# Strassen skips that end in the states' PSUM group, a planner that replays its plans, and moved units in a hybrid attention kernel

## Chip, cores and metric

The kernel runs on one core of one Trainium2 chip. The metric is the device time of one execution in microseconds (us); less is better. Everything is float32. TensorE (PE) multiplies matrices into PSUM, VectorE (DVE), ScalarE (ACT) and GpSimd (POOL) do the elementwise work, and SyncE (SP) issues the DMA transfers.

## What is computed

The input is `X` of shape (4, 1024, 256): 4 batches, 1024 tokens, 256 features. Four residual blocks follow one another:

```
x = x + attention(layernorm(x))          # causal, one head of 256
x = x + mix(layernorm(x))
x = x + state_space(layernorm(x))        # 16 states
x = x + mix(layernorm(x))                # the same weights again

mix(x):  xr, xk = blends of x with the token before, by mu_r and mu_k
         out = sigmoid(xr @ W_r.T) * (square(relu(xk @ W_k.T)) @ W_v.T)

state_space(x):
    xn = layernorm(x) * ln_g + ln_b
    x_proj, z = split(xn @ W_in.T + b_in);  z = silu(z)
    B_proj = x_proj @ W_B.T * mean(dt)                # 16 states
    x_mean = causal convolution of B_proj with the decays
    y = (x_mean @ W_C.T + D_skip * x_proj) * z        # the skip is D_skip * x_proj
    return y @ W_out.T + b_out + x
```

## The kernel before, in words

The tokens are cut into 8 halves `j` of 512 tokens (batch `b = j // 2`). Activations are kept by features, as [128 partitions, 2, 512], so that one product of a weight block [128, 128] with 512 tokens fills one PSUM bank.

**A written order on TensorE, a planned one elsewhere.** The program does not emit its instructions directly. It fills a log (`Order`): `o.unit` is a piece of TensorE work, and the units run in the order in which they are logged; `o.op` is a piece of work for another engine or a DMA, with its needs and the engines that may do it. `Order.finish` (L179) gives each op a due time, computed backwards from the units, and then simulates the whole program (`_run`) for 20 plans of three parameters, each in up to 5 rounds. After a round, `_hurry` pulls forward the due times of what TensorE waited for in it (`self.waits`). The plan with the earliest simulated end is emitted. So the order on DVE, ACT, POOL and SP over the whole program depends on which plan wins. The planner knows PSUM as 4 single banks ("bank") and 2 pairs of banks ("pair"), and the time that DVE and POOL share a port as `port`.

**The stages.** Attention works by tiles `i` of 128 queries, 32 in all: scores `sc` (L1492), exponents, a turn by DRAM (`exps`, `pblocks`), the weighted sum `po` (L1597). `attend_prepare(n)` logs the layernorm of half `n`, its trip through DRAM (`rows_a`, `blocks_a`) and the transposes into `xa`; the loop over `i` calls it 8 or 12 tiles ahead. The first mix block (`mix1`, tiles ending in `_f`) is threaded between the tiles. Then come, by hand in one list: the gates z, the inputs of the states, the convolution (`pc`, L1798), which goes to DRAM as `m_dram` and comes back as `xmT`, and the skips and outputs, with the second mix block (`mix2`, tiles ending in `_g`) threaded behind. `outputs(j)` is the product with `W_out` for half `j` and logs the layernorm and blends that half `j` of `mix2` needs.

**Seven products.** A product of a 256x256 weight with a batch's two halves is eight block products. `seven_products` (L818) does it with seven by Strassen's scheme in Winograd's form: sums of weight blocks (`x_sums`) and of activations (`T1` to `T4`, from `stream_sums`) are multiplied, and DVE adds the products out of PSUM in a chain: `u1`, `u2`, `u3`, then the four result blocks. For the gates z of batches 1 to 3 it has the keys `zs1` to `zs3` (p_zs in the profile), for the skips `ss1` to `ss3` (p_ss), for the keys of `mix2` `gks0` to `gks2`. `all_gates` is an iterator over the gates and skips, and each step of `more_gates(n)` logs n of its units. Batch 0 does its skips plainly: `skip(0)` and `skip(1)` (L1848) open an accumulation in a pair of banks, and `mix_states(0)` (L1925) adds the states' share `W_C` there and closes it.

**The states' share.** For batches 1 to 3 `mix_states_apart(b)` (unit `pm{b}`, L1889) multiplies `xmT` with `w_c` on four row groups at once into two pairs. Then DVE adds the skip to it (`grown`, L1899), and POOL or DVE multiplies with z (`gated`, L1903).

Of the kernel before, what the change touches and what calls it, by code (L numbers as in the profile page):

```python
# [4 lines left out]

# [10 lines left out]
ALU = mybir.AluOpType  # L16
# [36 lines left out]
class Order:  # L53
# [23 lines left out]
        for share, margin in ((0.2, 2.5), (0.1, 1.5), (0.3, 4.0), (0.2, 1.5), (0.1, 2.5))  # L77
        for wait in (0.0, 0.08, 0.15, 0.22)
    ]
    ROUNDS = 5  # L80
    TRIALS = 4
    BANKS = {"bank": 4, "pair": 2}
# [95 lines left out]
    def finish(self):  # L178
        dues = self._due()  # L179
        self.made = {e["key"]: n for n, e in enumerate(self.log) if e["key"] is not None}  # L180
        self.ends = []
        best = math.inf
        for plan in self.PLANS:
            self.due = list(dues)
            for k in range(self.ROUNDS):
                used = list(self.due)
                end = self._run(plan, False)
                self.ends.append((end, k, plan))
                if end < best:
# [4 lines left out]
        self._run(plan, True)  # L194

    def _hurry(self, key, wait):

# [8 lines left out]
    def _run(self, plan, emits):  # L206
        self.SHARE, self.MARGIN, self.WAIT = plan
        self.emits = emits
        self.waits = []
        self.now = self.at = 0.0  # L210
        self.free, self.ready, self.offered = {}, {}, []
        self.queue = self.port = 0.0
        self.waiting = {}
        self.psum = {kind: [0.0] * k for kind, k in self.BANKS.items()}
        for n, e in enumerate(self.log):
            if e["kind"] == "op":
                self._enter(n)
            elif e["kind"] == "known":
                self._done(e["key"], e["time"])
            elif e["kind"] == "take":  # L220
                heapq.heappop(self.psum[e["takes"]])
            else:
                self._unit(e)
        while self.offered:
            self._step()
        return max(self.now, *self.free.values())
# [57 lines left out]
    def _step(self):  # L284
        self.at, k = self._first()
        time, n = self.offered.pop(k)
        e = self.log[n]
        end, _, engine, emit = self._way(time, n)
        engine, _, port = engine.partition("+")
        self.free[engine] = end  # L290
        if port or engine == "POOL":
            self.port = end
        if self.emits:
            emit()
        if e["frees"]:
            heapq.heappush(self.psum[e["frees"]], end + self.LAG)
        if e["moves"]:
            for k, work in enumerate(e["moves"]):
                issued = end - (len(e["moves"]) - 1 - k) * self.log[n]["cost"] / len(e["moves"])
                self.queue = max(self.queue, issued + self.FLIGHT) + work  # L300
            self._done(e["key"], self.queue + self.LANDING)
        else:
            self._done(e["key"], end + e["lag"])
# [46 lines left out]
def hybrid_kernel(  # L350
# [1515 lines left out]
    def skips_of_batch(b):  # L1866

        there = columns_of(2 * b) + columns_of(2 * b + 1)
        src = lambda h, xb=(xnT[2 * b], xnT[2 * b + 1]): xb[h]()
        for j in (2 * b, 2 * b + 1):  # L1870
            skips[j] = lazy(lambda j=j: cols(f"skip_{j}"))
        sb = [skips[2 * b], skips[2 * b + 1]]
        sums_of_batch(b + 1)
        yield from seven_products(
            f"ss{b}", f"zs{b}", wx_block, lambda k: x_sums[:, k - 1, :], src, sums_of_batch(b),
            lambda e, h: sb[h]()[:, e, :], lambda e: b_skip[:, e : e + 1],
            ["x_sums", "b_all"], there,
        )

    def mix_states_apart(b):  # L1880

        for h in range(2):
            py[2 * b + h] = lazy(lambda h=h: pair(f"py_{2 * b + h}"))

        def emit():
            for e in range(KC):
                for h in range(2):
                    k = 2 * e + h
                    nc.tensor.matmul(  # L1889
                        py[2 * b + h]()[:, ts(e, HALF)],  # L1890
                        lhsT=w_c[k * GRP : k * GRP + S, ts(e, P)],
                        rhs=xmT[b]()[k * GRP : k * GRP + S, ts(h, HALF)],
                        start=True,
                        stop=True,
                    )

        def grown(j, e):
            t = skips[j]()[:, e, :]
            nc.vector.tensor_add(t, py[j]()[:, ts(e, HALF)], t)  # L1899

        def gated(engine, j, e):
            t = z[j]()[:, e, :]
            engine.tensor_mul(t, t, skips[j]()[:, e, :])  # L1903

        o.unit(f"pm{b}", 1.0, ["w_c", f"xmT{b}"], emit, "pair", many=2)
        for h in range(2):
            j = 2 * b + h
            for e in range(KC):
                o.op(
                    f"g{e}.{j}", [f"pm{b}", f"ss{b}.c{e + 1}{h + 1}"],  # L1910
                    ("DVE", dve(HALF) + 0.03, partial(grown, j, e)),
                    frees="pair" if e else None,
                )
# [107 lines left out]
    for i in range(-2, NI):  # L2021
        first, second = mix_units(i)
        while scored < min(i + (2 if i < AHEAD_FROM else 3), NI - 1):
            scored += 1
            if scored % NT == 0:
                for _ in chain:
                    pass
            scores(scored)
            if scored >= TURNED_BY_DRAM:
                turn_by_dram(scored)  # L2030
        go_on(APART)
        for unit in first:
            unit()
        go_on(APART)
        if 0 <= i + 1 < TURNED_BY_DRAM:
            turn(i + 1)
        j, k = divmod(i + 4, 4)
        if i == 0:
            next(attend_transpose(1))
        if 0 < j < 2 * NB:  # L2040
            if k == 0 and j == 1:
                attend_prepare(2)
            for n in range(3, 2 * NB):

                if i == 4 * n - (12 if n % 2 and n > 2 * SEVEN_FROM else 8):
                    attend_prepare(n)
            if k == (1 if i < AHEAD_FROM else 0) and j < 2 * SEVEN_FROM:
                both(queries, j)
            if k == 3 and j % 2 == 1 and SEVEN_FROM <= j // 2 + 1 < NB:
                chain = queries_of_batch(j // 2 + 1)  # L2050
                behind = len(o.log)
        while valued < min(i + (3 if i < AHEAD_FROM else 4), NI - 1):
            valued += 1
            values(valued)
        go_on(APART)
        for unit in second:
            unit()
        go_on(APART)
        if i == 10:
            decay_powers([f"e{i}", "la", "dtc", "dtr"])  # L2060
        if i == 13:
            decay_table()
        if 20 <= i < 23:
            next(steps_of_weights)
        if i >= 0:
            weigh(i)
            go_on(APART)
            if i % NH == NH - 1:
                mix1.prepare(i // NH, by_hand=i == NI - 1)
# [67 lines left out]
    more_gates(4)  # L2137
    outputs(2)
    more_gates(4)
    mix_states_apart(2)  # L2140
    outputs(3)
    more_gates(3)
# [86 lines left out]
```

## Time and profile before

| | |
|---|---|
| median of 3 runs | 465.42 us (465.42 to 465.47) |
| the profiled execution | 465.0 us, its span 463.1 us |
| granted TensorE clock | 1.0 |
| PE / DVE / ACT / POOL busy | 456.0 / 390.2 / 220.8 / 143.1 us |
| moved by DMA | 69.44 MB, mean 150 GB/s |

Attention and the first mix block take about the first 280 us, the gates, states and convolution go to about 310 us, the skips, outputs and the second mix block fill the rest. In the profile a float32 product of [128, 128] with 512 columns appears as two matmul instructions. A row that says "x8" has merged eight instructions, its second number runs from the first start to the last modelled end, and its last matmul still drains while the next row's first one runs, so that the rows overlap. "A <- B" after a row in brackets is idle time and what ended it. L numbers are lines of the kernel.

### The profile page before, as it was taken

The numbers are of one execution on the slowest core, as the hardware profiler recorded it, in microseconds if no ns is written. First come the engines' busy times: TensorE is split into PE (matmuls) and PEld (weight loads), VectorE is DVE, ScalarE is ACT, GpSimd is POOL, SyncE is SP. The second block draws the span as 40 slices with busy tenths as digits, with TensorE's granted clock in tenths as the row PEclk, the third lists the DMA queues.
The fourth block names the chain that finished last, engine by engine and source line by source line (L and its number), as shares of the span: only waits on it lengthen the run. The fifth ranks groups of instructions, "written<-read, shape, count | busy, mean of one in ns | idle before, by whom it ended". The sixth has DMA issues, their size and how long they took to land.

```text
span 463.1 us, 6634 instructions
## 1 busy us (share of the span) xinstructions
PE 456.0 (98%) x2052; PEld 312.5 (67%) x2052; DVE 390.2 (84%) x931; ACT 220.8 (48%) x463; POOL 143.1 (31%) x149
## 2 busy tenths in 40 slices
PE   8999999999999999999999999999999999999996
PEld 5766785667786667786777775474565758675875
DVE  3687769899969999889999977459889999999962
ACT  3422414454342433333556567441458777664652
POOL 3000102112013213121271354962052616826340
PEclk9999999999999999999999999999999999999999
DMA  8047876848455763427866989603022024252442
GB/s 242 21 127 203 250 190 168 222 132 258 117 135 139 221 194 93 118 62 237 224 177 182 275 268 271 260 17 88 11 92 91 1 86 144 81 147 99 129 144 84
DMA packets 84915, 69.44 MB, mean 150 GB/s; under 512 B 20160, under 2 KB 82576, under 8 KB 84880
## 3 DMA queue, kind: packets, MB, share of 16 engines
q1 hardware_dynamic: 84064, 68.76, 50.8%
q10 hardware_dynamic: 816, 0.26, 0.2%
q8 instruction: 16, 0.26, 0.2%
q14 instruction: 19, 0.16, 0.1%
HBM read 40.54 MB, written 28.45 MB: 149 GB/s over the span
## 4 chain that ended last, share of the span: by engine, by line
PE 86%; DVE 8%; issue 2%; DMA 1%; POOL 1%; ACT 1%; SPq 0%; DVEq 0%; POOLq 0%
PE po L1597 13%; PE sc L1492 13%; PE pv L1464 5%; PE p_zs L830 4%; PE p_ss L830 4%; PE p_qs L830 2%; PE p_gks L830 2%; PE py L1848 2%; PE pc L1798 2%; PE dust L1282 1%; DMA blocks_a<-rows_a 1%; PE pr_g0.pr L881 1%; PE pb L1735 1%; PE pp_a0.pq L774 1%; PE pr_g0.pv L881 1%
## 5 line engine op out<-in xcount | busy, mean ns | idle before, releaser
L1597 PE MATMUL po<-v,prT 128*128 128x256 f32 x288 | 67.7, 380 | 0.1
L1492 PE MATMUL sc<-xa,q 128*128 128x512 f32 (+3 forms) x192 | 67.0, 486 | 0.0
L1597 PEld LDWEIGHTS po<-v,prT 128*128 128x128 f32 x288 | 54.2, 189 | 11.6 <-issue 2.6
L1513 ACT ACTIVATE pr<-pr,nmx 128x128 f32<-128x128 f32 (+7 forms) x32 | 24.7, 773 | 64.6 <-DVE pr L1508 57.7
L1492 PEld LDWEIGHTS sc<-xa,q 128*128 128x128 f32 x192 | 35.1, 190 | 24.5 <-issue 19.6
L1464 PE MATMUL pv<-wv,xa 128*128 128x257 f32 x128 | 32.9, 380 | 0.0
L642 POOL TENSOR_TENSOR rs_a<-ve_a,minus_half 128x4 f32<-128x4 f32 x7 | 7.1, 1010 | 76.8 <-DVE ve_a L629 76.8
L1044 POOL TENSOR_TENSOR x<-x,r_f 128x512 f32<-128x512 f32 x16 | 20.3, 1271 | 33.0 <-DVE r_f L1038 32.5
L642 POOL TENSOR_TENSOR rs_h<-ve_h,minus_half 128x8 f32<-128x8 f32 x8 | 13.2, 1647 | 52.5 <-DVE ve_h L631 52.5
L1464 PEld LDWEIGHTS pv<-wv,xa 128*128 128x128 f32 x128 | 23.6, 191 | 7.8 <-issue 3.6
L1508 DVE TENSOR_SCALAR_CACHE_REDUCE pr<-sc,v 128x128 f32<-128x128 f32 (+7 forms) x32 | 26.2, 818 | 1.1
L1550 DVE STREAM_TRANSPOSE prT<-pblocks 128x384 f32<-128x384 f32 (+7 forms) x30 | 23.8, 793 | 2.4 <-DMA pblocks<-exps 2.3
L642 POOL TENSOR_TENSOR rs_f<-ve_f,minus_half 128x4 f32<-128x4 f32 x8 | 8.4, 1053 | 47.1 <-DVE ve_f L629 28.8
L1044 POOL TENSOR_TENSOR x<-x,r_g 128x512 f32<-128x512 f32 x14 | 18.9, 1371 | 11.0 <-DVE r_g L1038 11.0
L1641 POOL TENSOR_TENSOR x<-x,bout_r 128x512 f32<-128x512 f32 x16 | 20.0, 1279 | 4.5 <-ACT x L1634 4.5
L1606 DVE SCALAR_TENSOR_TENSOR x<-po,rsm,x 128x256 f32<-128x256 f32 x32 | 15.0, 470 | 4.3 <-PE po L1597 3.8
L1474 DVE TENSOR_TENSOR v<-pv,bv_r 128x257 f32<-128x257 f32 x32 | 13.4, 418 | 5.6 <-PE pv L1464 5.6
L930 DVE SCALAR_TENSOR_TENSOR xr_g<-hT_g,mur,xr_g 128x512 f32<-128x512 f32 x16 | 17.3, 1112 | 0.0
L663 ACT ACTIVATE xn_f<-x,mrs_f,rs_f 128x256 f32<-128x256 f32 x18 | 9.8, 592 | 15.5 <-DVE mrs_f L651 15.5
L1634 ACT ACTIVATE x<-x,mrs_h,rs 128x256 f32<-128x256 f32 x32 | 16.9, 592 | 0.0
L1903 POOL TENSOR_TENSOR z<-z,skip 128x512 f32<-128x512 f32 x9 | 13.1, 1462 | 10.9 <-DVE skip L1899 10.7
L663 ACT ACTIVATE xn_g<-x,mrs_g,rs_g 128x256 f32<-128x256 f32 x23 | 12.4, 589 | 8.3 <-DVE mrs_g L626 6.7
(458 smaller groups left out, 1089.8 us busy)
## 6 DMA issues: line engine op xcount, KB each, us to landing
hk<-r_dram SPq DMA_DIRECT2D x16, 512.0 KB, 9.2
rows_g<-xn_g SPq DMA_DIRECT2D x8, 512.0 KB, 2.9
blocks_g<-rows_g SPq DMA_DIRECT2D x32, 128.0 KB, 2.8
x<-in_L_attn_a_X_dram SPq DMA_DIRECT2D x7, 512.0 KB, 4.9
rows_f<-xn_f SPq DMA_DIRECT2D x7, 512.0 KB, 3.0
blocks_f<-rows_f SPq DMA_DIRECT2D x28, 128.0 KB, 2.7
rows_h<-xn_h SPq DMA_DIRECT2D x7, 512.0 KB, 3.7
blocks_h<-rows_h SPq DMA_DIRECT2D x28, 128.0 KB, 3.2
```

The costliest lines, as they stand in the source:

```text
L642: nc.gpsimd.tensor_tensor(rs()[:, :k].rearrange("p k n -> p (k n)"), ve()[:, :k].rearrange("p k n -> p (k n)"), minus_half[:, : k * NH], A ...
L663: nc.scalar.activation(place(n), split(row(n)), AF.Identity, bias=mrs()[:, k - 1, n : n + 1], scale=rs()[:, k - 1, n : n + 1],)
L830: lambda: nc.tensor.matmul(p(), lhsT=w(), rhs=data(), start=True, stop=True), "bank",
L930: nc.vector.scalar_tensor_tensor(t()[:, c, :], hT()[:, c, :HALF], mu1[:, c : c + 1], t()[:, c, :], ALU.mult, ALU.add,)
L1044: nc.gpsimd.tensor_add(xg, xg, r()[:, ts(g, 2), :])
L1464: nc.tensor.matmul(pv()[:, : D + 1], lhsT=xaj()[:, c, ts(n, P)], rhs=wv[:, c, :], start=(c == 0), stop=(c == KC - 1),)
L1492: nc.tensor.matmul(sc()[:, k * HALF : k * HALF + w], lhsT=qh()[:, c, ts(n, P)], rhs=keys[k]()[:, c, :w], start=(c == 0), stop=(c == KC - 1),)
L1508: nc.vector.tensor_scalar(dst, src, v[2 * b + h]()[:, n, D : D + 1], None, ALU.add, ALU.min, accum_out=nmx(),)
L1513: nc.scalar.activation(p()[:, :nk], p()[:, :nk], AF.Exp, bias=nmx(), scale=-1.0, accum_out=sm())
L1550: nc.vector.transpose(dst()[:, : NH * width].rearrange("p (k m a) -> p k m a", m=NH, a=GRP), blocks().rearrange("p m (k a) -> p k m a", a= ...
L1597: nc.tensor.matmul(po()[:, :D], lhsT=src()[:, ts(n, P)], rhs=v[2 * b + n // NH]()[:, n % NH, :D], start=(n == 0), stop=(n == t),)
L1641: nc.gpsimd.tensor_add(xg, xg, bout_r.unsqueeze(1).to_broadcast([P, 2, D]))
```

## The change

**The skips of batches 1 to 3.** `skips_of_batch` no longer runs all seven products. It runs four (1, 6, 7 and 5), and DVE makes from them `u1`, `u2 = u1 + p6`, `u3 = u2 + p7`, `u5 = u3 + p5` and `u4 = u2 + p5`, written straight into the four blocks of `skip`. The other three products (2, 4 and 3) move into the unit `pm{b}` of `mix_states_apart`, where each opens the accumulation group of one result block in the pairs; the states' share is then added onto it in PSUM. The fourth block has no product of its own and is opened by the states' share. `grown` then adds PSUM, the bias and the block `u` in one instruction. As the skips now have 4 steps instead of 7, all counts of `more_gates` change.

**The planner.** After each simulated run, the plan is replayed six times in its fixed order with varied durations (DVE up to 3% longer, ACT up to 4%, POOL up to 25%, each DMA landing up to 0.6 us later). The mean end of the replays decides between plans, and the waits averaged over the replays are what `_hurry` works on.

**Places.** `attend_prepare(n)` for n = 4 to 7 is logged one tile earlier. `skip(0)` moves from behind `state_inputs(1)` to ahead of `state_transpose(7)`. `mix2.gates(3, 0)` moves from behind the seven keys' products of batch 1 to between the fourth and the fifth; `mix2.gates(3, 1)` stays behind the seventh.

```diff
@@ class Order
+    SAMPLES = 6
+    SPREAD = {"DVE": 0.03, "ACT": 0.04, "POOL": 0.25}
+    LATE = 0.6
...
-                end = self._run(plan, False)
+                self._run(plan, False)
+                end = self._replays()
...
+    def _replays(self):
+        lost, ends = {}, 0.0
+        for k in range(self.SAMPLES):
+            rng = random.Random(k)
+            ends += self._replay(rng, lost)
+        self.waits = [(key, t / self.SAMPLES) for key, t in lost.items() if t > 0.1 * self.SAMPLES]
+        return ends / self.SAMPLES
+
+    def _replay(self, rng, lost):
...
+            spread = self.SPREAD.get(engine, 0.0)
+            at += cost * (1.0 + spread * rng.random())
...
+                at = queue + self.LANDING + self.LATE * rng.random()
...
@@ skips_of_batch(b)
-        yield from seven_products(
-            f"ss{b}", f"zs{b}", wx_block, lambda k: x_sums[:, k - 1, :], src, sums_of_batch(b),
...
+        u1, u2, u3, u5 = block(0, 0), block(0, 1), block(1, 0), block(1, 1)
+        p = unit(1, lambda: wx_block(0, 0), lambda: xnT[2 * b]()[:, 0, :], there)
+        o.op(f"{key}.u1", [f"{key}.p1"], *copies(u1, p), frees="bank")
+        yield
+        p = unit(6, lambda: x_sums[:, 1, :], lambda: T(2), [f"zs{b}.T2"])
+        add("u2", 6, p, u1, u2, "u1")
+        yield
+        p = unit(7, lambda: x_sums[:, 2, :], lambda: T(3), [f"zs{b}.T3"])
+        add("u3", 7, p, u2, u3, "u2")
+        yield
+        p = unit(5, lambda: x_sums[:, 0, :], lambda: T(1), [f"zs{b}.T1"])
+        add("u5", 5, p, u3, u5, "u3", last=False)
+        add("u4", 5, p, u2, u2, "u3")
+        yield
@@ mix_states_apart(b)
+            for h, e, w, data in (
+                (0, 0, wx_block(0, 1), xnT[2 * b]()[:, 1, :]),
+                (0, 1, wx_block(1, 1), T(4)),
+                (1, 0, x_sums[:, 3, :], xnT[2 * b + 1]()[:, 1, :]),
+            ):
+                nc.tensor.matmul(
+                    py[2 * b + h]()[:, ts(e, HALF)], lhsT=w, rhs=data, start=True, stop=False
+                )
...
-                        start=True,
+                        start=(k == 3),
...
-            nc.vector.tensor_add(t, py[j]()[:, ts(e, HALF)], t)
+            nc.vector.scalar_tensor_tensor(
+                t, py[j]()[:, ts(e, HALF)], b_skip[:, e : e + 1], t, ALU.add, ALU.add
+            )
...
-        o.unit(f"pm{b}", 1.0, ["w_c", f"xmT{b}"], emit, "pair", many=2)
+        o.unit(
+            f"pm{b}", columns(HALF, 3) + 1.05,
+            ["w_c", "x_sums", "b_all", f"xmT{b}", f"zs{b}.T4"] + there, emit, "pair", many=2,
+        )
@@ the loop over tiles
-                if i == 4 * n - (12 if n % 2 and n > 2 * SEVEN_FROM else 8):
+                if i == 4 * n - (12 if n % 2 and n > 2 * SEVEN_FROM else 8) - (n > 3):
                     attend_prepare(n)
@@ the list behind attention
     more_gates(5)
+    skip(0)
     state_transpose(7)
     state_inputs(0)
     more_gates(3)
     state_inputs_rows(0)
     state_inputs(1)
-    skip(0)
+    more_gates(2)
     state_inputs_rows(1)
-    more_gates(3)
+    more_gates(1)
...
     skip(1)
-    more_gates(8)
+    more_gates(6)
     mix_states(0)
-    more_gates(8)
+    more_gates(5)
     outputs(0)
-    more_gates(5)
+    more_gates(3)
     mix_states_apart(1)
     outputs(1)
-    more_gates(4)
+    more_gates(3)
     outputs(2)
-    more_gates(4)
+    more_gates(3)
     mix_states_apart(2)
     outputs(3)
     more_gates(3)
...
     outputs(7)
-    advance(keys, 7)
-    both(mix2.gates, 3)
+    advance(keys, 4)
+    mix2.gates(3, 0)
+    advance(keys, 3)
+    mix2.gates(3, 1)
```

More of the change, by code (lines that the diff above doesn't have):

```diff
@@ L2 @@
 import math
+import random
 from contextlib import ExitStack
@@ L194, in finish @@
         self._run(plan, True)
+    def _replays(self):
[6 more added lines that the diff above has]
+    def _replay(self, rng, lost):
+        now = queue = port = 0.0
+        free, ready = {}, {}
+        psum = {kind: [0.0] * k for kind, k in self.BANKS.items()}
+        for n, way in self.trail:
+            e = self.log[n]
+            if e["kind"] == "known":
+                ready[e["key"]] = e["time"]
+                continue
+            if e["kind"] == "take":
+                heapq.heappop(psum[e["takes"]])
+                continue
+            last, at = None, 0.0
+            for k in e["needs"]:
+                if ready[k] > at:
+                    last, at = k, ready[k]
+            if e["kind"] == "unit":
+                for _ in range(e["many"] if e["takes"] else 0):
+                    at = max(at, heapq.heappop(psum[e["takes"]]))
+                if last is not None and at > now + 0.1:
+                    lost[last] = lost.get(last, 0.0) + at - now
+                now = max(now, at) + e["cost"]
+                ready[e["key"]] = now + self.LAG
+                continue
+            engine, shared, cost = way
+            if e["moves"]:
+                at = max(at, queue - self.FLIGHT - 0.5)
+            at = max(at, free.get(engine, 0.0), port if shared or engine == "POOL" else 0.0)
+            spread = self.SPREAD.get(engine, 0.0)
+            at += cost * (1.0 + spread * rng.random())
+            free[engine] = at
+            if shared or engine == "POOL":
+                port = at
+            if e["frees"]:
+                heapq.heappush(psum[e["frees"]], at + self.LAG)
+            if e["moves"]:
+                for k, work in enumerate(e["moves"]):
+                    issued = at - (len(e["moves"]) - 1 - k) * e["cost"] / len(e["moves"])
+                    queue = max(queue, issued + self.FLIGHT) + work
+                at = queue + self.LANDING + self.LATE * rng.random()
+            else:
+                at += e["lag"]
+            if e["key"] is not None:
+                ready[e["key"]] = at
+        return max(now, *free.values())
     def _hurry(self, key, wait):
@@ L208, in _run @@
         self.emits = emits
-        self.waits = []
+        self.waits, self.trail = [], []
         self.now = self.at = 0.0
@@ L218, in _run @@
             elif e["kind"] == "known":
+                self.trail.append((n, None))
                 self._done(e["key"], e["time"])
             elif e["kind"] == "take":
+                self.trail.append((n, None))
                 heapq.heappop(self.psum[e["takes"]])
@@ L223, in _run @@
                 self._unit(e)
+                self.trail.append((n, None))
         while self.offered:
@@ L287, in _step @@
         e = self.log[n]
-        end, _, engine, emit = self._way(time, n)
+        end, start, engine, emit = self._way(time, n)
         engine, _, port = engine.partition("+")
+        self.trail.append((n, (engine, port, end - start)))
         self.free[engine] = end
@@ L1868, in skips_of_batch, with block, unit, add @@
         there = columns_of(2 * b) + columns_of(2 * b + 1)
-        src = lambda h, xb=(xnT[2 * b], xnT[2 * b + 1]): xb[h]()
+        key = f"ss{b}"
+        T = sums_of_batch(b)
         for j in (2 * b, 2 * b + 1):
             skips[j] = lazy(lambda j=j: cols(f"skip_{j}"))
-        sb = [skips[2 * b], skips[2 * b + 1]]
         sums_of_batch(b + 1)
-        yield from seven_products(
-            f"ss{b}", f"zs{b}", wx_block, lambda k: x_sums[:, k - 1, :], src, sums_of_batch(b),
-            lambda e, h: sb[h]()[:, e, :], lambda e: b_skip[:, e : e + 1],
-            ["x_sums", "b_all"], there,
-        )
+        def block(e, h):
+            return lambda: skips[2 * b + h]()[:, e, :]
+        def unit(r, w, data, need):
+            p = lazy(lambda: bank(f"p{r}_{key}"))
+            o.unit(
+                f"{key}.p{r}", columns(HALF), ["x_sums", "b_all"] + need,
+                lambda: nc.tensor.matmul(p(), lhsT=w(), rhs=data(), start=True, stop=True), "bank",
+            )
+            return p
+        def add(name, r, p, more, to, need, last=True):
+            o.op(
+                f"{key}.{name}", [f"{key}.p{r}", f"{key}.{need}"],
+                ("DVE", dve(HALF) + 0.03, lambda: nc.vector.tensor_add(to(), p(), more())),
+                frees="bank" if last else None,
+            )
[13 more added lines that the diff above has]
+        yield
     def mix_states_apart(b):
@@ L1883, in mix_states_apart @@
             py[2 * b + h] = lazy(lambda h=h: pair(f"py_{2 * b + h}"))
+        T = sums_of_batch(b)
         def emit():
+            for h, e, w, data in (
[6 more added lines that the diff above has]
+                )
             for e in range(KC):
@@ L1898, in grown @@
             t = skips[j]()[:, e, :]
-            nc.vector.tensor_add(t, py[j]()[:, ts(e, HALF)], t)
+            nc.vector.scalar_tensor_tensor(
+                t, py[j]()[:, ts(e, HALF)], b_skip[:, e : e + 1], t, ALU.add, ALU.add
+            )
         def gated(engine, j, e):
@@ L1903, in gated @@
             engine.tensor_mul(t, t, skips[j]()[:, e, :])
-        o.unit(f"pm{b}", 1.0, ["w_c", f"xmT{b}"], emit, "pair", many=2)
+        there = columns_of(2 * b) + columns_of(2 * b + 1)
+        o.unit(
+            f"pm{b}", columns(HALF, 3) + 1.05,
+            ["w_c", "x_sums", "b_all", f"xmT{b}", f"zs{b}.T4"] + there, emit, "pair", many=2,
+        )
         for h in range(2):
@@ L1909, in mix_states_apart @@
                 o.op(
-                    f"g{e}.{j}", [f"pm{b}", f"ss{b}.c{e + 1}{h + 1}"],
+                    f"g{e}.{j}", [f"pm{b}", f"ss{b}." + (("u1", "u4"), ("u3", "u5"))[e][h]]
+                    + ([f"ss{b}.u2"] if (e, h) == (0, 0) else [])
+                    + ([f"ss{b}.u5"] if (e, h) == (1, 0) else []),
                     ("DVE", dve(HALF) + 0.03, partial(grown, j, e)),
```

## The prediction, made before the changed kernel was run

> **What bounds the kernel now.** I read the page first, then the waits of TensorE, then its timeline row by row, because a wait shorter than the drain of the last matmul is not counted as idle. The page says that TensorE is busy all but 7 us, and that VectorE comes second:
>
> ```profile
> span 463.1 us, 6634 instructions
> PE 456.0 (98%) x2052; PEld 312.5 (67%) x2052; DVE 390.2 (84%) x931; ACT 220.8 (48%) x463; POOL 143.1 (31%) x149
> ```
>
> Of the 7.1 us of idle time the waits name 3.2, and 1.2 of these are the start, which the change leaves alone:
>
> ```profile
> PE dust L1282 <- DVE idle L427: 1.2, 1, 1.2
> PE p_gks L830 <- DVE u_gks L765: 1.0, 1, 1.0
> PE pr_g2.pr L881 <- ACT r_g L1016: 0.7, 1, 0.7
> PE pp_a0.pq L774 <- DVE xa L765: 0.3, 1, 0.3
> ```
>
> Another 3.7 us are the end, where the last row of products (at 455.72, 3.65 long) is out at 459.4 and the sums and stores follow. Is the busy time full speed? The timeline of TensorE tells it: eight instructions of 256 columns should take 1.73 us from start to start, four of 512 columns 1.72 (rows from 389.65 to 391.38 and 420.90 to 422.62). What is more than that is lost, shown as idle or not:
>
> ```profile
> 389.65 1.89 PE L881 MATMUL pr_pyo0.6_3520<-w_out,z 128*128 128x256 f32 x8
> 391.38 1.89 PE L881 MATMUL pr_pyo1.6_3533<-w_out,z 128*128 128x256 f32 x8
> 393.10 1.89 PE L881 MATMUL pr_g2.pr<-w_r,xr_g 128*128 128x256 f32 x8
> 395.68 1.99 PE L881 MATMUL pr_g2.pr<-w_r,xr_g 128*128 128x256 f32 x8 [0.69 <-ACT r_g L1016]
> ...
> 420.90 1.88 PE L830 MATMUL p_gks<-xk_g,w_fk 128*128 128x512 f32 x4
> 422.62 1.88 PE L830 MATMUL p_gks<-T_gks,fk_sums 128*128 128x512 f32 x4
> 425.48 1.10 PE L830 MATMUL p_gks<-T_gks,w_fk 128*128 128x512 f32 x2 [0.98 <-DVE u_gks L765]
> ```
>
> So 0.85 us are lost ahead of 395.68 and 1.14 ahead of 425.48, each with 0.1 more at the restart. Read in this way, the losses between 90 us and 430 us are: 92.89 (0.3, attention's `xa` late), 113.8 to 115.1 (0.5, banks), 176 to 182 (0.7, banks), 287 to 289 (0.3, `xn_h`), 358.4 (0.3), 362.2 (0.3), 377.1 (0.25), 395.7 (0.95), 425.5 (1.2). The sum is 4.8 us. This is all that any better order can return without taking work from TensorE.
>
> The stretches from the convolution on show who is behind these waits: VectorE is busy 97% from 350 to 378 and 97% from 400 to 430, and has air before them (32.44 of 37) and after (16.86 of 26 from 430 on).
>
> ```profile
> 313.00:350.00 37.00, 37.00 (x121) 20.13 (x120) 32.44 (x49) 15.43 (x49) 9.76 (x10) 1.00 0.20 59
> 350.00:378.00 28.00, 27.97 (x101) 17.45 (x100) 27.29 (x46) 21.68 (x67) 11.99 (x14) 1.00 0.17 56
> ...
> 400.00:430.00 30.00, 29.02 (x107) 19.81 (x106) 29.06 (x46) 18.24 (x32) 15.08 (x14) 1.00 0.45 140
> ```
>
> (Columns: sum of the stretch, then busy us of PE, weight loads, DVE, ACT, POOL, the clock, DMA.)
>
> **Rule against row, first.** The Trainium skill, "Perfetto Trace Analysis", section Identifying the Most-Contended Engine, says that matmul busy time is a bad measure of TensorE's headroom, and that the weight loads' busy share is a better one. Here that is 67%, which would leave a third of TensorE free and make VectorE the bound; the VectorE work saved below would then come off the end nearly one for one, some 6 us. But the starts above stand 0.215 and 0.43 us apart for the same shapes all along, with 4.8 us in excess. I take the row: the gain is capped at 4.8.
>
> **The skips, part by part.** TensorE: three products of 0.86 us for each of three batches move from `ss{b}` into `pm{b}`; none is saved, and the four small products at the end of `pm{b}` already add onto open groups in `mix_states(0)`, where they take 1.07 us as in the other batches. So 0. VectorE, from these rows:
>
> ```profile
> L840 DVE SCALAR_TENSOR_TENSOR skip<-p_ss,b_skip,u_ss 128x512 f32<-128x512 f32 x9 | 6.7, 744 | 0.5 <-issue 0.2 <-PE p_ss L830 0.2
> L1899 DVE TENSOR_TENSOR skip<-py,skip 128x512 f32<-128x512 f32 x10 | 6.6, 681 | 1.0 <-PE py L1889 1.0
> L840 DVE SCALAR_TENSOR_TENSOR skip<-p_ss,b_skip,skip 128x512 f32<-128x512 f32 x3 | 2.2, 747 | 0.1
> L838 DVE TENSOR_TENSOR u_ss<-p_ss,skip 128x512 f32<-128x512 f32 x3 | 2.1, 686 | 0.3 <-PE p_ss L830 0.2
> ```
>
> Before, a batch has four adds with bias (0.745 each) and three without (0.686); after, four without. `grown` goes from 0.68 to about 0.745, four times. Over three batches: 12 x 0.745 + 9 x 0.686 - 12 x 0.686 - 12 x 0.065 = 6.1 us less on VectorE, nearly all between 313 and 378. It lies beside TensorE, so it is worth only the waits it removes. Those at 358 (named `skip`), 362 and 377 (named `skip`) make 0.8; I take 0.6, as other adds remain.
>
> **The head start of the outputs.** With fewer skip units ahead, `outputs(0)` comes 5 units (16 to 11), that is 4.3 us, earlier on TensorE. `outputs(1)` gains 7 units less the 3 products now in `pm1`, 3.4 us; `outputs(2)` 4.3; `outputs(3)` and the next two 2.6. The layernorms and blends of `mix2` start that much earlier, while VectorE has 6.1 us less to do. The queue ahead of 395 and 425 should then be shorter by more than the 0.95 and 1.2 us lost there. I take 1.7 of these 2.15.
>
> **Rule against row, second.** The wait at 425 hangs on the copy `u_gks`, which stood in VectorE's queue behind these:
>
> ```profile
> 422.14 1.16 DVE mrs_g L651
> 423.30 1.44 DVE xn_g L657
> 424.74 0.61 DVE u_gks L765
> ```
>
> `mrs_g` on this line takes 0.12 us when undisturbed, `xn_g` 0.41; here 1.24 and 1.51, while POOL ran `T_gks` (421.67 to 423.28) and then added to `x`. "SBUF — State Buffer", section Who interferes with whom, says that VectorE and GpSimd share a port pair as an exclusive lock, taken by VectorE instructions with two SBUF inputs or in a two-port mode. The adds that this change removes have one input in PSUM, so by the rule the lock and its 2.2 us of delay stay, and the 1.2 us with them: the sum below would be 1.4 instead of 2.6. By the row the copy merely stood in a queue that had been full since 400 us, and with a shorter queue it is done earlier, lock or not. I take the row, and leave 0.45 for the rule.
>
> **A new wait.** Before `mix_states(0)` there are 6 units instead of 8. It starts 1.7 us earlier after `skip(1)`, at about 318.4 instead of 320.14. It needs the four loads of `xmT` for batch 0, the last of which is issued by SP at 315.83 and lands 2.7 us later (the median of these loads), at 318.5. So the slack of 1.6 us is used up: 0 to 0.5 us, and I take 0.2. Behind it TensorE's queue holds the last gates of batch 2 and `outputs(0)`, which now follows 4.3 us behind instead of 7; two instructions of 0.74 us gate its input, which fits if they go first. Unit `pm1` needs its pairs free and its `xmT` (last issue at 318.40) some ten us later: 0.
>
> **The moved units.** `skip(0)`, 3.6 us, stands ahead of the transposes at 287.87, so that `xn_h` has that much longer: 0.2 of 0.3 back. It is not longer in front of `pbt`, where gates stand instead: 0. The moved `gates(3, 0)` gives VectorE 1.7 us to empty banks between the keys' products; the row at 406.99 was only 0.1 late: 0. If its `xr_g` were late it would wait, but that is finished at 402.9, ahead of 404.4.
>
> **Attention's rows.** For halves 4 to 7, everything behind `attend_prepare` moves one tile (some 6 us) up: per half 4 statistics, 4 normalizations, one write of 512 KB and four reads of 128 KB on SP's queue (2.9 and 2.8 us to landing), 2 transposes. The same work, earlier; the wait at 92.89 should go: 0.3. What they are moved past on SP are the round trips of the exponents. Around 62 us, one such trip kept VectorE waiting 2.0 us, and its `po` began 2.6 us after the turn. If two halves' transfers landed there, 0 to 3 us; their new place, at tiles 7 and 15, comes ahead of short tiles with turns many us early (turned at 65.7, used at 78): 0.
>
> **The planner.** No row shows what another plan costs. It can at best return the bank waits at 114 and 176 (1.2 us). At worst it adds such waits all over attention, 0.33 us each by the row at 114.75 (0.30, and 0.1 on restart in some). With 32 tiles, half of them hit, that is 5.3 us. The replays punish plans with narrow margins, so I take 0, with both ends in the range.
>
> **The sum.** -0.6 - 1.7 + 0.2 - 0.2 - 0.3 = -2.6 us, on the profiled execution of 465.0 us (span 463.1): 462.4. The median of the runs is 0.4 above that execution, so 462.8.
>
> **The rivals.**
> - *The new plan costs bank waits in attention.* VectorE is busy 126.84 of 140 us between 60 and 200, so there is little room for putting hurried work ahead of the instructions that free PSUM. For it speaks that the whole order may change, and that attention now loses less than 2 us; against it, that the judging is made sterner. At half the tiles: 465.4 - 2.6 + 5.3 = 468.1. It decides against the change from 8 waits of 0.33 us; from 11 it is measurably slower. Chance 0.32.
> - *The wait for `xmT` takes the place of those removed,* together with the lock at 425: 2.6 becomes 2.6 - 1.2 - 0.3 = 1.1, which with one or two new bank waits ends at 464.3 to 465. For it: the slack computed above is nil. Chance 0.15.
> - *The planner does nothing with the earlier rows,* because a transfer is held back until 30 us ahead of its due time anyway. Then only 0.3 is lost: 463.1. This lies in the forecast.
> - The forecast, 460.7 (every wait gone) to 464.3: chance 0.53.
>
> About 0.2%, 0.9 us, is what a measurement of this kernel can tell from no change. The forecast and a third of the second rival's 0.15 lie below 464.5: 0.58 faster; the rest of that rival lies within: 0.10; the first rival is the 0.32 slower. For 8 in 10 I leave out nearly nothing below 460.7, and above 468, where more than half the tiles would have to wait, about 0.15. The forecast's own range is 460.7 to 464.3.
>
> **What would show it.** Right: PE's busy time within 1 us of 456.0; 12 `grown` of 0.74 and no p_ss add with bias; VectorE about 384 us; `pyo0.0` at about 324; the rows at 395 and 425 without gaps; the `xa` at 92 early. Wrong: bank waits (`x`, `v`, `r_f`) between 60 and 280 us above 2 us in sum, a gap ahead of L1925 above 0.5 us, or the gap ahead of `p_gks` still there.

## The result: slower by a third of a per cent

| | before | after |
|---|---|---|
| median | 465.20 us (20 runs, 463.96 to 466.53) | 466.07 us (20 runs, 465.14 to 470.06) |
| ratio | | 1.0036, 95% interval 1.0020 to 1.0052 |
| profiled execution, its span | 465.0, 463.1 us | 465.71, 463.9 us |

462.8 us and a faster kernel were predicted. The changed kernel is slower: it lies outside the forecast's own range (460.7 to 464.3) and inside the wide one (460.7 to about 468), on the side of the first rival. The 20 executions of after do not lie evenly. Twelve had a mean granted clock of 0.998 or more and took 465.14 to 466.28 us; eight had 0.996 or less and took 467.27 to 470.06. These eight are why the ratio is larger than that of the medians (1.0019). What stands behind them is told under the experiments.

The page of after. VectorE's sum is what the prediction said it would be (383.2 us, about 384 forecast). TensorE's is 1.7 us below the 456.0 of before, where the prediction allowed 1:

```profile
span 463.9 us, 6625 instructions
PE 454.3 (98%) x2052; PEld 312.1 (67%) x2052; DVE 383.2 (83%) x923; ACT 223.3 (48%) x467; POOL 136.0 (29%) x143
```

VectorE's groups in the skips (line, operation, shapes, count, then busy us, mean ns, and idle time before them). The adds with a bias on `p_ss` are gone, and `grown` carries the bias now:

```profile
L2001 DVE SCALAR_TENSOR_TENSOR skip<-py,b_skip,skip 128x512 f32<-128x512 f32 x12 | 8.5, 738 | 0.9 <-PE py L1991 0.9
L1954 DVE TENSOR_TENSOR skip<-p_ss,skip 128x512 f32<-128x512 f32 x12 | 8.1, 686 | 3.1 <-PE p_ss L1947 2.7 <-issue 0.2
```

TensorE's waits are another list than before. `pr_g2.pr` is gone from it. `pt_h7.T` is new, as long as the wait of the start (`dust`, 1.2 us), and `p_gks` stands twice. Four of its rows:

```profile
PE pt_h7.T L821 <- DVE xn_h L722: 1.2, 1, 1.2
PE p_gks L895 <- DVE ka_g L903: 1.0, 1, 1.0
PE pp_g6.pk L839 <- ACT ka_g L1029: 0.7, 1, 0.7
PE p_gks L895 <- DVE T_gks L878: 0.7, 1, 0.7
```

TensorE's timeline at two places that the prediction named:

```profile
324.02 1.24 PE L946 MATMUL pr_pyo0.0_3037<-w_out,z 128*128 128x256 f32 x5
...
392.99 3.19 PE L946 MATMUL pr_g2.pr<-w_r,xr_g 128*128 128x256 f32 x14
```

`pr_pyo0.0` starts at 324.02, as forecast, and the blends at 392.99 run through without the gap that stood at 395.68. The product with `xmT` (318.55) waits for nothing. But there are gaps ahead of 291.39 (`pt_h7.T`), 402.43 and 426.07 (`p_gks`) and 440.90 (`pp_g6.pk`). The gap ahead of `p_gks` was one of the prediction's own signs of being wrong.

**Where the time went.** From each instruction of TensorE to the next I took the distance of the starts, less 0.215 us (256 columns) or 0.43 us (512 columns), and summed what was over 0.04 us too much. This counts each change of shape too (about 0.1), so that even a stretch without waits shows some tenths:

| lost on TensorE, us | 85 to 285 | 285 to 300 | 300 to 350 | 350 to 450 | sum |
|---|---|---|---|---|---|
| before | 1.04 | 0.62 | 0.59 | 3.49 | 5.74 |
| after | 0.72 | 2.00 | 0.77 | 3.99 | 7.47 |

That is 1.7 us more. The count leaves out the distances behind small products. There a bank wait at 114.75 (0.28 us) went, and the one of 0.17 at 176.82 became 0.55 at 175.59 (`po`, behind `b_rows`), which adds 0.1. The first product of attention's queries, at 12.84 us before, came 1.1 us earlier in the profile of after. In later profiles of before's plan it came at 12.23 and 12.53 (`e13`, `e14`), so I count the 1.1 as an accident of the start. 1.7 + 0.1 - 1.1 = 0.7, as between the two profiled executions.

### The profile page after: what moved, and what is told of

Its sections match the earlier page's. It is cut to its first block, busy times and chain, and to the rows that moved or that the text cites. A ratio compares the mean times of both kernels' runs of the same rounds, so it can differ in the third digit from the quotient of the medians.

```text
span 463.9 us, 6625 instructions
## 1 busy us (share of the span) xinstructions
PE 454.3 (98%) x2052; PEld 312.1 (67%) x2052; DVE 383.2 (83%) x923; ACT 223.3 (48%) x467; POOL 136.0 (29%) x143
## 4 chain that ended last, share of the span: by engine, by line
PE 75%; DVE 12%; DMA 5%; POOL 2%; issue 2%; ACT 2%; SPq 2%; DVEq 0%; POOLq 0%
PE po L1662 14%; PE sc L1557 13%; PE pv L1529 6%; PE p_zs L895 3%; DMA blocks_g<-rows_g 3%; PE p_qs L895 3%; PE pc L1863 2%; PE p_ss L1947 1%; SPq L790 1%; DVE xr_g L995 1%; DMA rows_g<-xn_g 1%; DVE xk_g L995 1%; DVE skip L2001 1%; DVE hT_g L796 1%; DMA wq<-in_L_attn_a_Wq_dram 1%
## 5 line engine op out<-in xcount | busy, mean ns | idle before, releaser
L1109 POOL TENSOR_TENSOR x<-x,r_g 128x512 f32<-128x512 f32 x14 | 17.6, 1272 | 9.4 <-DVE r_g L1103 9.0
L728 ACT ACTIVATE xn_h<-x,mrs_h,rs_h 128x256 f32<-128x256 f32 x21 | 11.4, 591 | 17.0 <-DVE mrs_h L716 17.0
L728 ACT ACTIVATE xn_g<-x,mrs_g,rs_g 128x256 f32<-128x256 f32 x20 | 10.9, 591 | 15.5 <-DVE mrs_g L691 12.7
L796 DVE STREAM_TRANSPOSE hT_g<-blocks_g 128x512 f32<-128x512 f32 x16 | 10.7, 696 | 7.7 <-DMA blocks_g<-rows_g 7.7
L728 ACT ACTIVATE xn_f<-x,mrs_f,rs_f 128x256 f32<-128x256 f32 x20 | 10.8, 591 | 12.3 <-DVE mrs_f L716 12.3
```

What stands on the lines that cost most here:

```text
L728: nc.scalar.activation(place(n), split(row(n)), AF.Identity, bias=mrs()[:, k - 1, n : n + 1], scale=rs()[:, k - 1, n : n + 1],)
L1109: nc.gpsimd.tensor_add(xg, xg, r()[:, ts(g, 2), :])
```

## What happens at half 7

The largest new loss is at 287 to 291 us, ahead of the last transposes in front of the convolution. Timeline of after, rows of POOL, VectorE and TensorE (start, duration; "x3" is three instructions in a row):

```profile
287.02 3.77 POOL L1706 TENSOR_TENSOR x<-x,bout_r 128x512 f32<-128x512 f32 x3
287.08 1.29 DVE L716 SCALAR_TENSOR_TENSOR mrs_h<-rs_h,mv_h 128x4 f32<-128x4 f32 x2 [1.76 <-POOL rs_h L707]
288.30 3.36 DVE L722 TENSOR_SCALAR xn_h<-x,mv_h,rs_h 128x256 f32<-128x256 f32 x3
...
291.39 1.19 PE L821 MATMUL pt_h7.T<-ident,xn_h 128*128 128x128 f32 x7 [1.18 <-DVE xn_h L722]
```

The same place before:

```profile
285.75 1.27 POOL L1641 TENSOR_TENSOR x<-x,bout_r 128x512 f32<-128x512 f32 x1
286.71 0.41 DVE L651 SCALAR_TENSOR_TENSOR mrs_h<-rs_h,mv_h 128x4 f32<-128x4 f32 x2
287.04 1.05 DVE L657 TENSOR_SCALAR xn_h<-x,mv_h,rs_h 128x256 f32<-128x256 f32 x3
```

Before, one add of POOL stands behind `rs_h`, and `xn_h` starts within 0.02 us of its end. After, three adds stand there. The two `mrs_h` of 128x4 take 1.29 us instead of 0.41, and the three `xn_h` 3.36 instead of 1.05. `skip(0)` on TensorE (286.51 to 290.11) gives them 3.6 us that they did not have before, and TensorE still waits.

**Theory P (the port).** VectorE waits while POOL adds, for the whole of an add: the lock that the prediction weighed at 425 us and set aside. The new plan put three adds under `xn_h`. **Rival S (the skips and the places).** The moved work itself makes things late. **Rival J (the judging).** Plans chosen by replays are worse than those chosen by one simulation. The first set takes the change apart, the second draws plans without the change, and the third tests P alone.

## First set: the parts alone

`e1_skips_only` has the skips' change with its counts of gates in the list, and neither the replays nor the moved rows and units:

```diff
-        yield from seven_products(f"ss{b}", f"zs{b}", wx_block, ...
+        p = unit(1, lambda: wx_block(0, 0), lambda: xnT[2 * b]()[:, 0, :], there)
...
-    more_gates(8)
+    more_gates(6)
     mix_states(0)
```

> The skips' change alone: four products and three in the states' unit, with the counts of the gates that go with it; the old judging of plans and the old places. If the skips' change is sound and the loss comes from the replays or the places, this is faster than before by 1.5 to 2.5 us (0.995), VectorE's busy time falls by about 6 us, and the outputs of half 0 start about 4.3 us earlier. If the three products in the states' unit themselves cost time, it is slower by 1 us or more with the loss between 313 and 385 us. If every other log just draws another plan, it lands anywhere within 2 us of before, and its losses are at other places than those of the changed kernel.

`e2_replays_only` has only the judging:

```diff
-                end = self._run(plan, False)
+                self._run(plan, False)
+                end = self._replays()
```

> The judging by replays alone, on the log of before: no instruction is added or removed, only the orders on VectorE, ScalarE, GpSimd and SyncE can change. If the plan that replays choose is what lost the time, this is slower than before by 1.5 us or more (1.003 to 1.006). If replays are sound and the places are at fault, it is the same or up to 1 us faster. If the plan is a draw, within 2 us on either side, with waits of TensorE at new places.

`e3_places_only` has only attention's rows, `skip(0)` and the other moved units:

```diff
-                if i == 4 * n - (12 if n % 2 and n > 2 * SEVEN_FROM else 8):
+                if i == 4 * n - (12 if n % 2 and n > 2 * SEVEN_FROM else 8) - (n > 3):
...
+    skip(0)
     state_transpose(7)
```

> The moved places alone (attention's rows one tile earlier, skip(0) ahead of the transposes of half 7, the gates of half 3 split), old judging and old skips. If the places are at fault, slower by 1 us or more, with the wait ahead of the transposes of half 7 (1.3 us in the changed kernel) in its profile. If not, the same or faster by up to 0.8 us and no such wait, since skip(0) gives the normalization 3.4 us more.

`e4_no_replays` is after with the judging of before:

```diff
-                self._run(plan, False)
-                end = self._replays()
+                end = self._run(plan, False)
```

> The changed kernel with the old judging of plans: skips and places changed, no replays. If the replays' choice is at fault, this is faster than before by 2 us or more (0.996 or less) and the waits at 291, 402, 426 and 441 us are gone. If skips or places are at fault, it is as slow as the changed kernel (1.003 to 1.005). If the plan is a draw, within 2 us on either side.

| | median, us (runs) | ratio to before, 95% |
|---|---|---|
| e1_skips_only | 468.58 (4) | 1.0082 [1.0069, 1.0095] |
| e2_replays_only | 467.06 (6) | 1.0050 [1.0032, 1.0068] |
| e3_places_only | 467.25 (6) | 1.0051 [1.0036, 1.0066] |
| e4_no_replays | 467.37 (6) | 1.0055 [1.0041, 1.0068] |

The three parts cost 1.8% in sum, and 0.36% together: costs that add up do not look like this. e2 has nothing of S in it, e4 nothing of J, and both are slower than before, so neither can be the whole of it. e1 lost 3.8 us, more than its expectation allowed for another draw, and not between 313 and 385 us. The losses lie at other places each time. e1 and e4 have long `xn_h` at half 7 (2.96 and 3.36 us for three). e3 has it worst (3.92 us). e2 has not (1.05 us), but lost 2.5 us at 159.6 us to an attention `xa` that was late. That wait occurs in no other profile here, and I did not follow it up.

## Second set: plans that mean nothing

If any edit draws another plan, an edit without meaning must do it too. `e5_null_vector` and `e6_null_scalar` are before, with one nanosecond more in the planner's own estimate of a VectorE or a ScalarE instruction. `e7_other_draws` is after with other random numbers in the replays.

```diff
--- e5
-    return 0.02 + n / 850
+    return 0.021 + n / 850
--- e6
-    return 0.22 + n * 0.72e-3
+    return 0.221 + n * 0.72e-3
--- e7, against after
-            rng = random.Random(k)
+            rng = random.Random(k + 100)
```

> The kernel before, with the planner's cost of every VectorE instruction set 1 ns higher (0.021 + n/850 instead of 0.020 + n/850) and nothing else: the same instructions, but another plan may win. If before has an ordinary plan and each part of the change really costs its 2 to 4 us, this is the same as before within 0.7 us. If before's plan is an unusually good draw, this is slower by 1 to 4 us as the four runs with one part each were, with TensorE's waits at new places.

> The kernel before, with the planner's cost of every ScalarE instruction set 1 ns higher (0.221 instead of 0.220) and nothing else. A second draw of the same kind: within 0.7 us of before if its plan is ordinary; 1 to 4 us slower if its plan is an unusually good draw.

> The changed kernel with other random numbers in the replays (seeds 100 to 105 instead of 0 to 5) and nothing else. If the changed kernel's 1.0036 is owed to its parts, this is the same within 0.7 us. If it is owed to the plan drawn, it is another number, anywhere from 462 to 469 us, and the waits at 291, 402, 426 and 441 us are replaced by others.

e5: 465.06 us (13 runs), ratio 1.0004 [0.9995, 1.0014]. e6: 472.33 us (4 runs), **1.0150** [1.0135, 1.0165]. e7: 467.33 us (6 runs), 1.0042 [1.0026, 1.0057]. A nanosecond in an estimate cost 7 us, by the ratios four times what the change under study did. (e5's plan is another one too, but its three `xn_h` took 1.06 us.) With such a spread, one plan with replays and one without cannot tell whether replays choose better. The timeline of e6 shows four adds over the same normalizations:

```profile
286.51 5.04 POOL L1641 TENSOR_TENSOR x<-x,bout_r 128x512 f32<-128x512 f32 x4
287.79 3.91 DVE L657 TENSOR_SCALAR xn_h<-x,mv_h,rs_h 128x256 f32<-128x256 f32 x3
```

**A second price.** In the profile of e6 the clock falls behind this wait. Two stretches of its windows, ahead of the fall and in it (columns: the stretch and its us, then busy us of PE, weight loads, DVE, ACT and POOL, the granted clock, DMA):

```profile
287.70:291.19 3.49, 1.89 (x6) 0.53 (x4) 3.49 (x5) 2.63 (x5) 3.49 (x4) 1.00 0.99 316
291.19:294.60 3.41, 2.85 (x13) 1.33 (x17) 3.38 (x6) 2.06 (x5) 1.17 (x3) 0.50 1.02 419
```

The profiles of e3 (from 299.63) and e7 (from 263.21) show the same, behind 3.4 us in which TensorE was busy for 1.41 and 1.12 us. In these three, 3.4 us in which TensorE was busy for 1.1 to 1.9 us were followed by 3.41 us at a clock of 0.50. It does not always come. The profile of e2 has a stretch as thin, and its clock stayed at 1.00:

```profile
156.20:159.60 3.40, 0.99 (x6) 0.54 (x4) 3.34 (x7) 1.24 (x2) 0.00 (x0) 1.00 0.97 246
159.60:163.00 3.40, 3.40 (x12) 2.38 (x13) 3.37 (x6) 1.59 (x4) 1.01 (x1) 1.00 0.28 79
```

What decides is not shown. By these figures such a window costs 1.7 us of work (half of 3.41), and 1.7 / 463 takes the mean clock from 1.0 to 0.996. That is the clock of all four runs of e6 and of seven of the longer eight of after (the eighth had 0.993); no run of before shows less than 0.998. The Trainium skill, "TensorE: Matmul & The Clock Gate", section HAM oscillation, warns of idle gaps above some 3.4 us. Here single waits of 0.6 to 2.6 us in a thin stretch were enough in three profiles, and one of 2.5 us (e2) was not. Where in after the window falls is not shown: its profiled execution had none.

## Third set: the same plans with other POOL queues

What tells P from all the rest is to keep a plan and move only POOL's adds. `e9_held_adds` is after, with the adds of `bout_r` that come due behind `rs_h` of half 7 issued behind the clearing of `bp`. The orders of the other engines are those of after.

```diff
         def powers(n0, n1):
+            hold[0] = hold[0] or key == "h7"
...
-            nc.gpsimd.tensor_add(xg, xg, bout_r.unsqueeze(1).to_broadcast([P, 2, D]))
+            add = partial(nc.gpsimd.tensor_add, xg, xg, bout_r.unsqueeze(1).to_broadcast([P, 2, D]))
+            if hold[0]:
+                held.append(add)
+                return
+            for late in [add] + held:
+                late()
+            held.clear()
...
                 nc.gpsimd.memset(bp()[:, :, : NT - 1, :], 0.0)
+                hold[0] = False
```

> The changed kernel with its plan kept: only three adds of the output's bias on GpSimd, which run from 287.0 to 290.8 us, are emitted behind the clearing of bp, some 10 us later. The order on TensorE, VectorE, ScalarE and SyncE is the same to the instruction. If the port that VectorE shares with GpSimd makes xn_h of half 7 late, the three xn_h take about 1.05 us instead of 3.36 and mrs_h 0.25 instead of 1.29, the wait of 1.3 us ahead of the transposes is gone, no run loses TensorE's clock there, and the time falls by 1.4 to 2.5 us to about before's. If xn_h is late for another reason (the transposes of xnT ahead of it that wait for a DMA), xn_h stays late and the time stays within 0.5 us of the changed kernel's.

464.21 us (13 runs, 463.75 to 464.95), ratio **0.9983** [0.9974, 0.9992]: faster than before, and 0.53% (2.5 us) below after. Its timeline at half 7:

```profile
287.11 0.47 POOL L1836 MEMSET bp<- 128x448 f32 x1
287.20 0.24 DVE L719 SCALAR_TENSOR_TENSOR mrs_h<-rs_h,mv_h 128x4 f32<-128x4 f32 x2 [1.76 <-POOL rs_h L710]
287.35 1.06 DVE L725 TENSOR_SCALAR xn_h<-x,mv_h,rs_h 128x256 f32<-128x256 f32 x3
```

`xn_h` is done at 288.41, 1.9 us ahead of the transposes (290.34). The loss between 285 and 300 us falls from 2.00 to 0.39, and no run has a clock below 0.998. 1.6 us come from the wait. The rest of the 2.5 fits the halved clock: eight of 20 runs, each 2.6 us longer in the mean, make 1.0 us. That is worked out and not shown. The clearing on POOL (`MEMSET`), which only writes, runs over `mrs_h` and does not delay it. It seems to hold an `xn_h`, though: the second one of after took 1.75 us and ended 0.15 us behind the clearing (291.34, 291.19), and the traces of e4 show the same.

`e10_skips_held` and `e11_no_replays_held` do the same to e1 and e4, and `e13_lock_in_before` does the opposite to before: three adds on a dead array behind `rs_h`, nothing else.

```diff
--- e13, against before, in powers()
+            if key == "h7":
+                for _ in range(3):
+                    nc.gpsimd.tensor_add(wv[:, :, :D], wv[:, :, :D], wv[:, :, :D])
```

> The skips' change and the new pair counts alone, as in the earlier run that measured 468.6 us, with one thing more: POOL's adds of bout_r to x that come due after rs_h of half 7 are issued behind the clearing of bp. Only POOL's order differs. If the shared port under xn_h of half 7 was this plan's cost (there 0.6 + 1.15 us of waits at 287 to 289), it ends 1.3 to 3 us earlier: 465.6 to 467.3. If the waits further on (404 to 442 us, some 4 us in sum) were the cost and would have absorbed those at 287, it stays at 468 to 469.

> The changed kernel with the old way of judging plans (measured 467.4 us), again with POOL's late adds of bout_r held until bp is cleared; only POOL's order differs. Port theory: the wait of 1.13 us ahead of the transposes of half 7 goes, 465.3 to 466.4. Rival, that this plan is slow only by its waits of 0.5 to 1 us between 406 and 440: 467.0 to 467.6, no change.

> The kernel before in its own plan, with three adds of 128x512 on POOL, on an array that is dead by then, put right behind rs_h of half 7: no engine's order changes but for these. Port theory: xn_h of half 7 goes from 1.05 to 1.3 us or more, mrs_h from 0.4 to 1.2; TensorE waits 1 us or more ahead of the transposes of half 7: 466.3 to 468.5. Rival, that the lock is harmless here since the transposes were late for another reason: 465.2 to 465.6.

e13: 467.38 us (6 runs), 1.0060 [1.0040, 1.0081]. Three adds that no other engine waits for cost 2.5 us:

```profile
285.25 3.28 POOL L650 TENSOR_TENSOR wv<-wv 128x512 f32<-128x512 f32 x3
287.43 2.85 DVE L660 TENSOR_SCALAR xn_h<-x,mv_h,rs_h 128x256 f32<-128x256 f32 x3
...
290.01 1.20 PE L759 MATMUL pt_h7.T<-ident,xn_h 128*128 128x128 f32 x7 [1.43 <-DVE xn_h L660]
```

Two of its six runs (469.23 and 469.31) have a clock of 0.996, as in after. e10: 467.20 us (6 runs), 1.0047 [1.0034, 1.0060], against 1.0082 without the hold. e11: 466.33 us (13 runs), 1.0027 [1.0014, 1.0039], against 1.0055. In both, `xn_h` is back at 1.05 us, and the loss from 285 to 300 us went from 2.21 to 0.39 and from 1.68 to 0.39. That makes 1.8 and 1.3 us by the losses, 1.6 and 1.3 by the ratios. So P holds in four plans (of after, e1, e4 and before). It is not all: e10 still loses 6.1 us between 350 and 450 us, nearly as e1 (6.2), and stays slower than before.

## The second place: 425 us

The prediction weighed the lock at 425 us and decided for a full queue. `e12_gated` is e9, and the adds of `r_g` to `x` wait for the last `xn_g` of half 6 too, by a copy of one column. `e14_before_gated` puts the same gate into before.

```diff
-                nc.gpsimd.tensor_add(xg, xg, r()[:, ts(g, 2), :])
+                gated_add(partial(nc.gpsimd.tensor_add, xg, xg, r()[:, ts(g, 2), :]))
...  in gated_add, once the last xn_g of g6 is emitted
+            nc.gpsimd.tensor_copy(wv[:, 0, :1], gate[0]())
```

> The changed kernel with the held adds (464.2 us), and in addition POOL's adds of r_g to x made to wait for the last xn_g of g6, by a copy of one column on POOL; the orders of the other engines stay. Port theory for the second place: xn_g near 424 falls from 1.5 to 0.4 us each, and the wait of 0.95 us near 424.5 goes: 463.2 to 463.6. Rival, a queue of VectorE that is full there whatever the port does: the wait stays or moves by a few us, 464.0 to 464.6.

> The kernel before in its own plan, with POOL's adds of r_g to x made to wait for the last xn_g of g6 by a copy of one column on POOL, as in the run that measured 463.3 us on the changed kernel. Port theory: xn_g near 423 falls from 1.5 to 0.4 us, u_gks comes 1 us earlier, the gap of 0.98 us ahead of 425.5 goes and the time falls by 0.7 to 1.1 us, to about 464.0; the changed kernel with both edits then keeps a lead of 0.6 to 1 us that is the skips' own. Rival, a queue of VectorE that is full there: no change, 464.8 to 465.3, and the lead is 1.6 us.

e12: **463.27 us** (14 runs, 462.20 to 464.44), ratio 0.9965 [0.9953, 0.9977], the fastest version here (its interval and that of e9 just overlap). First after, then e12:

```profile
422.74 1.26 POOL L1109 TENSOR_TENSOR x<-x,r_g 128x512 f32<-128x512 f32 x1
422.89 1.14 DVE L716 SCALAR_TENSOR_TENSOR mrs_g<-rs_g,mv_g 128x4 f32<-128x4 f32 x1
423.95 1.47 DVE L722 TENSOR_SCALAR xn_g<-x,mv_g,rs_g 128x256 f32<-128x256 f32 x1
```

```profile
423.29 0.13 DVE L740 SCALAR_TENSOR_TENSOR mrs_g<-rs_g,mv_g 128x4 f32<-128x4 f32 x1
423.34 0.41 DVE L746 TENSOR_SCALAR xn_g<-x,mv_g,rs_g 128x256 f32<-128x256 f32 x1
```

`ka_g`, next in the queue, starts at 423.66 instead of 425.34 (0.4 us of this was there at 402 already), and the losses from 350 to 450 us fall from 3.55 (e9) to 2.00. `p_gks` is gone from TensorE's waits. (In five of the 14 runs the clock is 0.996, 464.14 to 464.44 us; the profile has such a run, with the halved stretch at 12.25 us, in the start that all these kernels share. The other nine took 462.20 to 463.80.) So in the changed kernel the copy and its successors at 425 were late by the port and not by the queue's length.

e14: 465.19 us (14 runs), 1.0009 [0.9999, 1.0018]: no gain. The time is what the rival expected, but not for its reason, for the gap did go:

```profile
424.35 0.40 DVE L679 TENSOR_SCALAR xn_g<-x,mv_g,rs_g 128x256 f32<-128x256 f32 x1
...
434.74 1.31 DVE L755 STREAM_TRANSPOSE hT_g<-blocks_g 128x512 f32<-128x512 f32 x2 [1.48 <-DMA blocks_g<-rows_g]
...
442.80 1.99 PE L905 MATMUL pr_g6.pr<-w_r,xr_g 128*128 128x256 f32 x8 [0.47 <-DVE r_g L1062]
```

In this profile TensorE came to 425 us with 1.2 us of delay, from a DMA that landed late at 287. The gap that went made that good (the product stands at 425.52, before at 425.48). But the rows of half 6 were on their way with the whole delay, since `mrs_g` ahead of them is still locked, by the POOL product `T_gks` (1.25 us here too). They landed 1.5 us later than before, and TensorE lost 0.8 us more between 438 and 443 instead. So in this execution the wait moved to the next thing that was late. It took 466.08 us, 0.9 above the median of the 14; where the others, without the late DMA, lost the gain is not shown. How much of e12's lead over before is due to the skips' change itself therefore stays open: e12 and e14 differ in plan as well.

## Why the prediction was wrong, point by point

The largest step that failed is the planner, put at 0: three POOL adds that the new plan placed under `xn_h` cost 2.5 us (e9), nearly as much as the whole gain that was forecast (2.6). In us on TensorE, as forecast and as the table of losses has it (350 to 450 is split between the first two steps by the waits that they named; what the new plan cost stands in the rows where it fell):

| step | forecast | measured |
|---|---|---|
| skips' waits at 358, 362, 377 | -0.6 | -0.4 (0.4 is left at 356.19) |
| head start of the outputs | -1.7 | +0.9 |
| wait for `xmT` | +0.2 | 0 |
| `skip(0)` ahead of the transposes | -0.2 | +1.4 |
| attention's rows | -0.3 | -0.3 |
| 300 to 350 | 0 | +0.2 |
| sum | -2.6 | +1.7 (before rounding) |

*Right:* VectorE lost 7.0 us of work (6.1 forecast), `grown` takes 0.738 us (0.745), `pyo0.0` starts at 324.02, the `xa` at 92 is early, `xmT` costs nothing.

*"The planner: 0" failed.* The step priced another plan by bank waits in attention alone, -1.2 to +5.3 us. The bank waits did not come (85 to 285 us: 0.72 after 1.04, and 0.1 more behind small products), so the first rival named the right sign by a wrong mechanism. That the result lies in the wide range is luck. Two edits that mean nothing moved the kernel by 0 and by +7 us. Of the eight other plans that ran here with POOL's queue as planned, seven were slower, by 0.4 to 1.5%, and one was level.

*"skip(0) ... 0.2 back" failed.* The step gave `xn_h` 3.6 us and looked at TensorE's side alone. What else stood in POOL's queue behind `rs_h` was not asked: three adds there made 0.2 back into 1.4 lost.

*"I take the row" failed, at the lock.* By the Trainium skill, "SBUF — State Buffer", section Who interferes with whom, the lock stays since the adds that go have an input in PSUM. e12 shows that the rule was right at 425 us: without POOL's adds beside it `xn_g` took 0.41 us instead of 1.47, and the wait was gone. e13 shows that the same lock elsewhere (2.5 us) is dearer than the place at which I priced it (1.2).

*The head start failed*, beside the lock, for a second reason, argued from the windows of after (columns as above):

```profile
313.00:350.00 37.00, 37.00 (x127) 19.82 (x126) 28.46 (x49) 16.52 (x52) 6.54 (x9) 1.00 0.19 57
350.00:378.00 28.00, 27.88 (x103) 19.11 (x103) 27.44 (x48) 22.43 (x70) 10.89 (x12) 1.00 0.18 57
...
400.00:430.00 30.00, 28.34 (x103) 18.93 (x102) 28.26 (x52) 18.26 (x32) 13.63 (x12) 1.00 0.32 104
```

VectorE's work fell by 4.0 us between 313 and 350, where it had air before (32.44), rose by 0.15 between 350 and 378 (27.29), and fell by 0.8 between 400 and 430 (29.06). The prediction saw that the stretches from 350 and from 400 were the full ones, and still counted work saved ahead of them as a shorter queue in them.

## What to carry to other kernels

Where an order comes from a planner, an edit and a new draw of the plan arrive together: run a null edit first to see how far a draw alone moves the time (here 0 to 7 us), and compare with a plan held still. An engine that is busy for 29% of the time, POOL here, can still set the end: before an operation that TensorE waits for, look at what stands in POOL's queue beside it, and hold back what nobody needs. And a gap that is removed can be lost again at the next late arrival, as in the profile of e14; count work saved in the stretch where it was short, not ahead of it.

## What the runs showed of the hardware

- Behind an add of POOL (128x512, 1.26 us), a VectorE operation of 128x4 took 1.14 us instead of 0.13, and a normalization of 128x256 1.37 instead of 0.40. POOL's own adds were hardly longer (3.77 us for three, 2.52 for two). In these traces it is VectorE that waits, for the whole of POOL's instruction; in e3 two adds of POOL took 1.72 us each instead of 1.27.
- TensorE's clock was halved for one stretch of 3.41 us behind stretches of the same length in which it was busy for a third to somewhat over a half of the time (e3, e6, e7), without a single wait as long as that. In e12 the halved stretch at the start (12.25 us) stands behind 3.44 us with 2.78 busy. In e6 three waits of 2.7 us in sum (289 to 292 us) had an estimated 1.7 us more behind them. A stretch busy for 0.99 of 3.40 us in e2 had no such thing behind it, and in the one plan of e13 two of six runs show the lower clock.
